# The first row tiles asked for by two queues, and the query weights in four transfers behind a hold

## The chip, the cores and the metric

The kernel runs on one core of one Trainium2 chip. The metric is the device time of one execution in microseconds. The kernel before took 1141.29 us, the median of three runs (1140.83 to 1142.23).

## The reference: what is computed

The input is x, 2 x 2048 rows of 512 float32 values. Two sublayers follow each other, each as x = x + layernorm(f(layernorm(x))).

The first, f, is an attention over 64 fixed latent keys with 16 heads of 32 values:

```
Q = h @ Wq.T + bq ;  V = h @ Wv.T + bv
logits = Q . latent / sqrt(32)              (64 for each head and row)
the best 4 of the 64, softmax over these 4, sum of their latent rows
out = (that sum + V) @ Wo.T + bo
```

The second is a gated expert layer of 2048 hidden values, silu(h @ Wu.T) * (h @ Wg.T), then @ Wd.T. Its three weight matrices are made ternary first: scale = mean(|W|) over the whole matrix, W = clip(round(W / scale), -1, 1) * scale. So every piece of such a matrix has to be read once for its scale before any piece of it can be used.

## The kernel before, in words

The 4096 rows are worked on in eight blocks of 512 rows, each of four tiles of 128 rows. All weights are loaded once and stay on the chip. While block b goes through the experts on TensorE, the attention of block b + 1 is worked in between by all engines. The start is different: nothing is there yet. Its order is written out by hand in FIRST_STEPS (line 36 on), a list of step names that is carried out from left to right. The table STEPS (line 856) says which function each name calls. The tile framework does not reorder anything; each engine takes its instructions in the order in which the steps issue them, and waits by semaphores.

What happens in the first 70 us, with the names that are used below:

- load_x(0) (line 129) asks for the four row tiles of block 0, 256 KB each, by SyncE's queue. Then one transfer for wq, the query weights (1024 KB, line 161), follows.
- Sixteen matmuls of ones (line 186) keep TensorE busy from the start. Their results go to at_psum, a PSUM pool of two buffers, and are not used.
- ast t takes the statistics of a row tile on VectorE (bn_stats and bn_aggr, lines 249 and 250). ars computes the reciprocal deviation on GpSimd (lines 256 and 257). aap t normalizes the tile on VectorE (line 276). atr t transposes it on TensorE in four pieces (line 286). acp t copies the transposed tile from PSUM to hT, by ScalarE for tiles 0 to 2 and by VectorE for tile 3 (lines 568 to 571).
- hold (line 852) stands behind ast0 in the list. It writes one column of lk by VectorE and then calls load_weights (line 163), which asks by SyncE's queue for lk, the biases, wv, lv, bo, the row tiles of block 1, and then the raw expert weights in pieces: eight of raw_u, four of raw_g, wo, four of raw_g, ten of raw_d. Because the first of these transfers writes lk, it waits for that VectorE write, and all the others stand behind it in the same queue.
- q c makes query tile c on TensorE (line 577, four matmuls over wq) into acc_psum, a pool of four buffers. qc copies it out on ScalarE (line 592) after bh, which copies bo (line 650). l makes the logits (line 602), lc copies them (line 610).
- su, sg, sd i sum the absolute values of one raw piece on ScalarE (line 206). tot adds the sums up on TensorE (line 214), sc makes the scale on VectorE, rd rounds a piece on GpSimd, and sgu, sgg and the like take its sign on ScalarE (line 237).
- m and r find the best four logits of a head on VectorE (lines 385 to 397), e and n make the weights of them.

There is one more order to know of. The transfers share eight queue semaphores in turn, so a transfer may have to wait until the one eight places before it has landed.

Of the kernel before, what the change touches and what calls it, by code (L numbers as in the profile page):

```python
# [17 lines left out]
P = 128  # L18
# [14 lines left out]


FIRST_STEPS = """
ast0 hold ast1 ars0_2 ast2 ars2_3 ast3 ars3_4 aap0 aap1 atr0 aap2 atr1 acp0 aap3 atr2 acp1 atr3 acp2 acp3 q0 bh
q1 qc0 bl nst0 l0 nst3 qc1 su0 nst1 v0 lc0 nst2 lc1 nrs su2 m1 su3 m0 l1 su1 r0 q2 lc2 su5 nap0
e0 r1 su6 ntr0 qc2 q3 ncp0 nap3 su7 nap1 nap2 sg1 n0 sg2 ob0 ob1 m2 ob2 e1 v1 qc3 n1 lc3 sg4 r2
t0 t1 tc0 ob3 tc1 sg5 m3 ntr2 e2 ntr1 ncp2 r3 y0 ncp1 l2 yc0 sg7 o3_0 n2 e3 o2_0 sd0 n3 v3 lc5
# [19 lines left out]
def latent_attention_ternary_glu(  # L59
# [15 lines left out]
    nc = tc.nc  # L75
    NT, D = x_in.shape
    E = wuT.shape[1]
    DC = D // P
# [18 lines left out]
    def at_psum(name):  # L97
        return ps_at.tile([P, 512], F32, tag="at", name=name)
# [11 lines left out]
    def transposed(which, b, name, dtype):  # L110
        return work.tile([P, DC, TB], dtype, tag=f"{which}{b % 2}", name=name, bufs=1)
# [17 lines left out]
    def load_x(b):  # L129
        x_tiles[b] = []  # L130
        for t in range(TT):
            xt = work.tile([P, D], F32, tag="x", name=f"x_{b}_{t}", bufs=2 * TT)
            r = b * TB + t * P
            nc.sync.dma_start(out=xt, in_=x_in[r : r + P, :])
            x_tiles[b].append(xt)


# [8 lines left out]
    def load_up(n, src, pieces):  # L146
        for i in pieces:
            k, h = halves[i]
            nc.sync.dma_start(
                out=raw[n, i], in_=src[k * P : (k + 1) * P, h * CH : (h + 1) * CH]  # L150
            )

    load_x(0)
    wq = wpool.tile([P, DC, D], F32, name="wq")
    wv = wpool.tile([P, DC, D], F32, name="wv")
# [2 lines left out]
    bo_sb = wpool.tile([P, D], F32, name="bo_sb")  # L158
    lk = wpool.tile([P, DC, 2 * L], F32, name="lk")
    lv = wpool.tile([P, H // 2, HP], F32, name="lv")  # L160
    nc.sync.dma_start(out=wq, in_=wqT.rearrange("(c p) n -> p c n", p=P))

    def load_weights():
        nc.sync.dma_start(out=lk, in_=latk)
        nc.sync.dma_start(out=bqv_sb, in_=bqv)
        nc.sync.dma_start(out=wv, in_=wvT.rearrange("(c p) n -> p c n", p=P))
        nc.sync.dma_start(out=lv, in_=latv)
        nc.sync.dma_start(out=bo_sb, in_=bo.to_broadcast([P, D]))
        load_x(1)
        load_up("u", wuT, (0, 2, 3, 1, 5, 6, 7, 4))  # L170
        load_up("g", wgT, (1, 2, 4, 5))
        nc.sync.dma_start(out=wo, in_=woT.rearrange("(c p) n -> p c n", p=P))
        load_up("g", wgT, (7, 6, 0, 3))
        for i in (0, 2, 3, 6, 7, 9, 8, 1, 5, 4):
            rows = 2 * P if i < 6 else P
            r = i * 2 * P if i < 6 else 12 * P + (i - 6) * P
            nc.sync.dma_start(
                out=raw["d", i].rearrange("p (c n) -> p c n", n=D),
                in_=wdT[r : r + rows, :].rearrange("(c p) n -> p c n", p=P),
            )  # L180
# [2 lines left out]
    both = work.tile([P, 2, P], F32, tag="hid", name="ones", bufs=2)  # L183
    ones = both[:, 0, :]
    nc.vector.memset(ones, 1.0)
    for i in range(16):
        nc.tensor.matmul(at_psum(f"ones_{i}")[:, :P], lhsT=ones, rhs=ones, start=True, stop=True)
    ident = wpool.tile([P, P], F32, name="ident")
    make_identity(nc, ident)
# [93 lines left out]
    def transpose_row(h, name, psum=at_psum):  # L283
        pt = psum(f"pt_{name}")
        for c in range(DC):
            nc.tensor.transpose(pt[:, c * P : (c + 1) * P], h[:, c * P : (c + 1) * P], ident)
        return pt.rearrange("p (c k) -> p c k", k=P)
# [252 lines left out]
    class FirstAttention(Attention):  # L540
# [19 lines left out]
        def a_trans_pe(self, t):  # L560
            if self.hT is None:
                self.hT = transposed("X", self.b, f"hT_{self.b}", F32)
            self.pt = getattr(self, "pt", {})
            self.pt[t] = transpose_row(self.rows.pop(("a", t)), f"a{self.b}_{t}")

        def a_copy(self, t):
            dst, src = self.hT[:, :, t * P : (t + 1) * P], self.pt.pop(t)
            if self.b == 0 and t == 3:
                nc.vector.tensor_copy(dst, src)
            else:  # L570
                nc.scalar.copy(dst, src)
# [277 lines left out]
        return work.tile([P, TB], F32, tag=tag, name=f"qT_0_{c}", bufs=2)  # L849


    def hold_weights():
        nc.vector.memset(lk[:, 0, 0:1], 0.0)
        load_weights()

    STEPS = {
        "ast": A.a_stats,
# [6 lines left out]
        "l": A.l_pe,  # L864
        "lc": A.l_copy,
        "hold": hold_weights,
        "m": A.m,
        "r": A.r,
# [151 lines left out]
    for b in range(NB):  # L1020
# [5 lines left out]
        for e in range(EC):  # L1026
            if e == 4 and 0 < b < NB - 1:
                load_x(b + 1)
# [136 lines left out]
```

## Time and profile before

| what | us |
|---|---|
| median of three runs | 1141.29 |
| the profiled execution, its whole time | 1141.65 |
| its span, first to last instruction | 1139.9 |
| TensorE busy | 1126.4 |
| first transpose of block 0 on TensorE (line 286) | 9.21 |
| first query matmul (line 577) | 12.48 |
| wq asked for, and us to landing | 2.57, 7.8 |
| the matmul that adds up raw_g's sums (line 214) | 69.15 |

Times in the views are microseconds from the start of the span. PE is TensorE's matmul, PEld its weight load, DVE is VectorE, ACT ScalarE, POOL GpSimd and SPq SyncE's queue. A row of the timeline gives start, length, engine, line, operation, what it writes and reads, its shape and how many such stood together; the bracket behind it is the idle time of the engine before it and what ended that. In the chain of waits each row is one link on the way back from the last instruction of the kernel: start, length, and the engine and line, or the transfer, in which the time passed. TensorE's granted clock is 0.999 of full in the whole span, in this profile.

### The profile page before, as it was taken

The numbers are of one execution on the slowest core, as the hardware profiler recorded it, in microseconds if no ns is written. First come the engines' busy times: TensorE is split into PE (matmuls) and PEld (weight loads), VectorE is DVE, ScalarE is ACT, GpSimd is POOL, SyncE is SP. The second block draws the span as 40 slices with busy tenths as digits, with TensorE's granted clock in tenths as the row PEclk, the third lists the DMA queues.
The fourth block names the chain that finished last, engine by engine and source line by source line (L and its number), as shares of the span: only waits on it lengthen the run. The fifth ranks groups of instructions, "written<-read, shape, count | busy, mean of one in ns | idle before, by whom it ended". The sixth has DMA issues, their size and how long they took to land.

```text
span 1139.9 us, 14491 instructions
## 1 busy us (share of the span) xinstructions
PE 1126.4 (99%) x4602; PEld 770.4 (68%) x4602; DVE 835.8 (73%) x2952; ACT 412.1 (36%) x715; POOL 164.8 (14%) x204
## 2 busy tenths in 40 slices
PE   8999999999999999999999999999999999999997
PEld 5547666767667665776657766586675766758885
DVE  5978968687866887678877778678786787846435
ACT  4985542332233332333214333153322433224223
POOL 1057003110032000320002200032001120020100
PEclk9999999999999999999999999999999999999999
DMA  9800221432213322222222222232321412102001
GB/s 350 305 0 21 73 94 41 108 120 84 83 52 97 102 86 81 73 76 93 93 74 75 83 95 96 60 103 65 117 68 56 111 65 93 63 3 74 37 1 37
DMA packets 98572, 97.16 MB, mean 85 GB/s; under 512 B 8384, under 2 KB 71104, under 8 KB 98496
## 3 DMA queue, kind: packets, MB, share of 16 engines
q1 hardware_dynamic: 98496, 96.24, 26.8%
q8 instruction: 36, 0.59, 0.2%
q14 instruction: 40, 0.33, 0.1%
HBM read 59.51 MB, written 36.70 MB: 84 GB/s over the span
## 4 chain that ended last, share of the span: by engine, by line
PE 94%; DVE 3%; ACT 1%; DMA 1%; issue 0%; SPq 0%; DVEq 0%; ACTq 0%
PE pg L716 20%; PE pu L716 19%; PE acc L759 19%; PE po L468 8%; PE pv L440 8%; PE pq L353 7%; PE pv L457 3%; PE pl L367 2%; PE pq L577 2%; PE po L668 1%; PE pv L622 1%; DMA hT<-far_a 1%; DMA x<-in_x 0%; PE pl L602 0%; DVE left L393 0%; ACT tern_g L237 0%
## 5 line engine op out<-in xcount | busy, mean ns | idle before, releaser
L716 PE MATMUL pg<-hT_f,tern_g 128*128 128x512 f32 x512 | 207.6, 405 | 0.0
L716 PE MATMUL pu<-hT_f,tern_u 128*128 128x512 f32 x512 | 204.7, 401 | 0.0
L759 PE MATMUL acc<-tern_d,hi 128*128 128x512 f32 x512 | 203.4, 397 | 0.0
L759 PE MATMUL acc<-tern_d,lo 128*128 128x512 f32 x512 | 199.8, 390 | 0.9 <-DVE lo L749 0.8
L716 PE MATMUL pg<-lT_f,tern_g 128*128 128x512 f32 x512 | 199.6, 390 | 0.0
L716 PE MATMUL pu<-lT_f,tern_u 128*128 128x512 f32 x512 | 198.9, 389 | 0.0
L725 ACT ACTIVATE h<-pu,columns 128x512 f32<-128x512 f32 x128 | 87.0, 680 | 203.5 <-PE pu L716 203.5
L728 DVE SCALAR_TENSOR_TENSOR h<-h,pu 128x512 f32<-128x512 f32 x128 | 85.9, 671 | 93.7 <-ACT h L725 93.7
L744 ACT CAST hi<-h 128x512 fp32r<-128x512 f32 x128 | 79.1, 618 | 199.2 <-DVE h L733 199.1
L733 DVE TENSOR_TENSOR h<-h,pg 128x512 f32<-128x512 f32 x128 | 86.4, 675 | 63.5 <-PE pg L716 62.3
L759 PEld LDWEIGHTS acc<-tern_d,hi 128*128 128x128 f32 x512 | 96.1, 188 | 32.9 <-issue 13.6
L716 PEld LDWEIGHTS pg<-hT_f,tern_g 128*128 128x128 f32 x512 | 96.1, 188 | 25.3 <-issue 1.4
L716 PEld LDWEIGHTS pu<-hT_f,tern_u 128*128 128x128 f32 x512 | 96.1, 188 | 25.1 <-issue 3.1
L759 PEld LDWEIGHTS acc<-tern_d,lo 128*128 128x128 f32 x512 | 96.1, 188 | 22.9 <-DVE lo L749 2.2
L716 PEld LDWEIGHTS pu<-lT_f,tern_u 128*128 128x128 f32 x512 | 96.2, 188 | 22.6 <-issue 3.1
L716 PEld LDWEIGHTS pg<-lT_f,tern_g 128*128 128x128 f32 x512 | 96.2, 188 | 21.7 <-issue 2.9
L749 DVE TENSOR_TENSOR lo<-h,hi 128x512 fp32r<-128x512 f32 x128 | 89.9, 702 | 23.1 <-ACT hi L744 23.1
L440 PE MATMUL pv<-hT,wv 128*128 128x512 f32 x224 | 100.7, 592 | 0.3 <-ACT w L375 0.3
L393 DVE MATCH_REPLACE8 left<-m,w 128x64 f32<-128x64 f32 x512 | 100.3, 210 | 0.0
L468 PE MATMUL po<-wo,attnT 128*128 128x512 f32 x224 | 97.3, 592 | 0.0
L353 PE MATMUL pq<-hT,wq 128*128 128x512 f32 x192 | 86.7, 594 | 0.5 <-DMA hT<-far_a 0.2
L468 PEld LDWEIGHTS po<-wo,attnT 128*128 128x128 f32 x224 | 42.5, 190 | 50.8 <-issue 48.6
(141 smaller groups left out, 1310.7 us busy)
## 6 DMA issues: line engine op xcount, KB each, us to landing
dz<-z SPq DMA_DIRECT2D x56, 256.0 KB, 2.0
wT<-dz SPq DMA_DIRECT2D x224, 64.0 KB, 1.9
x<-in_x SPq DMA_DIRECT2D x32, 256.0 KB, 3.7
out_x<-x SPq DMA_DIRECT2D x31, 256.0 KB, 2.0
far_f<-zf SPq DMA_DIRECT2D x28, 256.0 KB, 2.8
hw<-far_f SPq DMA_DIRECT2D x56, 128.0 KB, 3.4
xa<-in_x SPq DMA_DIRECT2D x6, 1024.0 KB, 5.3
far_a<-za SPq DMA_DIRECT2D x24, 256.0 KB, 2.9
```

The source lines that it names most:

```text
L353: nc.tensor.matmul(pq, lhsT=wq[:, k, c * P : (c + 1) * P], rhs=self.taken(k), start=(k == 0), stop=(k == DC - 1),)
L393: nc.vector.match_replace(left[:, g, :], m8[:, g, :], w[:, g, :], TAKEN)
L440: nc.tensor.matmul(self.pv[c], lhsT=wv[:, k, c * P : (c + 1) * P], rhs=self.ordered(k), start=(k == 0), stop=False,)
L457: nc.tensor.matmul(self.pv[c][pr * HP : (pr + 1) * HP, :], lhsT=lv[:, 2 * c + pr, :], rhs=self.wT.pop(2 * c + pr), start=False, stop=True, ...
L468: nc.tensor.matmul(self.po[t], lhsT=self.attnT[:, c, t * P : (t + 1) * P], rhs=wo[:, c, :], start=(c == 0), stop=(c == DC - 1),)
L716: nc.tensor.matmul(p, lhsT=tern[n, 2 * k + e // 8][:, (e % 8) * P : (e % 8 + 1) * P], rhs=self.parts[i][:, k], start=(k, i) == pairs[0], s ...
L725: nc.scalar.activation(self.h[e], self.pu[e], AF.Tanh, scale=half_u[0])
L728: nc.vector.scalar_tensor_tensor(self.h[e], self.h[e], 1.0, self.pu.pop(e), ALU.add, ALU.mult)
L733: nc.vector.tensor_tensor(self.h[e], self.h[e], self.pg.pop(e), ALU.mult)
L744: nc.scalar.copy(hi, self.h[e])
L749: nc.vector.tensor_tensor(lo, self.h.pop(e), self.hid[e][0].bitcast(F32), ALU.subtract)
L759: nc.tensor.matmul(self.acc[t], lhsT=part[:, t * P : (t + 1) * P], rhs=wd, start=(e == 0 and i == 0), stop=(e == EC - 1 and i == 1),)
```

## The change

Five edits, all in the first microseconds:

```
-ast0 hold ast1 ars0_2 ast2 ars2_3 ast3 ...
+ast0 hold0 ast1 ars0_2 ast2 hold1 ars2_3 ast3 ...
...
-            nc.sync.dma_start(out=xt, in_=x_in[r : r + P, :])
+
+            queue = nc.scalar if b == 0 and t % 2 else nc.sync
+            queue.dma_start(out=xt, in_=x_in[r : r + P, :])
...
-    nc.sync.dma_start(out=wq, in_=wqT.rearrange("(c p) n -> p c n", p=P))
-
-    def load_weights():
+    def load_weights(group):
+        if group == 0:
+            for k in range(DC):
+                nc.sync.dma_start(out=wq[:, k, :], in_=wqT[k * P : (k + 1) * P, :])
+            return
...
-    for i in range(16):
+    for i in range(20):
         nc.tensor.matmul(at_psum(f"ones_{i}")[:, :P], lhsT=ones, rhs=ones, start=True, stop=True)
...
-            self.pt[t] = transpose_row(self.rows.pop(("a", t)), f"a{self.b}_{t}")
+            psum = acc_psum if self.b == 0 and t >= 2 else at_psum
+            self.pt[t] = transpose_row(self.rows.pop(("a", t)), f"a{self.b}_{t}", psum)
...
-            if self.b == 0 and t == 3:
+            if self.b == 0 and t == 2:
                 nc.vector.tensor_copy(dst, src)
...
-    def hold_weights():
-        nc.vector.memset(lk[:, 0, 0:1], 0.0)
-        load_weights()
+    def hold_weights(group):
+        nc.vector.memset((lk if group else wq)[:, 0, 0:1], 0.0)
+        load_weights(group)
```

Row tiles 1 and 3 of block 0 are asked for by ScalarE's queue, where they stand ahead of its first activation table load; tiles 0 and 2 stay on SyncE's. The query weights come in four transfers of 256 KB, one for each 128 rows of the matrix, and the first of them waits for a VectorE write to wq that stands behind tile 0's statistics (hold0). The other weights wait for the write to lk, which now stands behind tile 2's statistics (hold1). There are 20 matmuls of ones, not 16. The transposes of tiles 2 and 3 go to acc_psum, and of the copies to hT it is tile 2's that VectorE makes, so that ScalarE makes tile 3's. Nothing else differs on any engine but the numbers of the queue semaphores.

More of the change, by code (lines that the diff above doesn't have):

```diff
@@ L35 @@
 FIRST_STEPS = """
-ast0 hold ast1 ars0_2 ast2 ars2_3 ast3 ars3_4 aap0 aap1 atr0 aap2 atr1 acp0 aap3 atr2 acp1 atr3 acp2 acp3 q0 bh
+ast0 hold0 ast1 ars0_2 ast2 hold1 ars2_3 ast3 ars3_4 aap0 aap1 atr0 aap2 atr1 acp0 aap3 atr2 acp1 atr3 acp2 acp3 q0 bh
 q1 qc0 bl nst0 l0 nst3 qc1 su0 nst1 v0 lc0 nst2 lc1 nrs su2 m1 su3 m0 l1 su1 r0 q2 lc2 su5 nap0
```

## The prediction

> **What bounds the kernel now.** I read the page first, then the chain of waits over the first 60 us, the timeline of the first 13 us, the DMA view, and last the places where an engine starts exactly when something lands.
>
> ```profile
> PE 1126.4 (99%) x4602; PEld 770.4 (68%) x4602; DVE 835.8 (73%) x2952; ACT 412.1 (36%) x715; POOL 164.8 (14%) x204
> ```
>
> TensorE is busy 1126.4 of 1139.9 us, so all its idle time is 13.5 us, and nothing in this diff shortens its useful work. The chain of waits, first 60 us (start, length, what):
>
> ```profile
> 1.63 5.27 DMA x<-in_x
> ...
> 6.92 0.71 DVE st_a L249
> ...
> 9.21 0.64 PE pt_a L286 x4
> ...
> 12.48 7.10 PE pq L577 x16
> ```
>
> The start waits for the third row tile: asked for at 1.63, landed at 6.90. From 12.48 on the chain is TensorE. The timeline of VectorE:
>
> ```profile
> 3.43 0.69 DVE L249 BATCH_NORM_STATS2 st_a<-x 128x6 f32<-128x512 f32 x1 [2.45 <-DMA x<-in_x]
> ...
> 4.29 0.06 DVE L853 MEMSET lk<- 128x1 f32 x1
> ...
> 6.92 0.69 DVE L249 BATCH_NORM_STATS2 st_a<-x 128x6 f32<-128x512 f32 x1 [1.75 <-DMA x<-in_x]
> ```
>
> Tile 0 is there at 3.4 and tile 1 by 4.26, then VectorE waits 1.75 us for tile 2. The wait is in transfers, not in their issue: the DMA view gives 2.7 us to landing for the first tile, 5.4 for those asked for last, and wq, asked for at 2.57, takes 7.8, so lands at 10.4. In the stages table the 16 DMA engines are busy 1.03 and 0.92 of the time from 4 to 6 us yet move only 281 and 219 GB/s, against 405 later (us, PE, PEld, DVE, ACT, POOL, clock, DMA share, GB/s):
>
> ```profile
> 5.00:6.00 1.00, 1.00 (x10) 0.99 (x9) 0.17 (x1) 0.00 (x0) 0.65 (x2) 1.00 0.92 219
> ...
> 20.00:40.00 20.00, 20.00 (x90) 10.46 (x86) 18.72 (x113) 18.66 (x38) 1.21 (x2) 1.00 1.03 405
> ```
>
> So packets of the last tiles and the first of wq are slow together, and the weight stream then runs full until 49 us. That stream matters more than the start:
>
> ```profile
> 20.21 1.05 ACT L206 ACTIVATE junk<-raw_u 128x1024 bf16<-128x1024 f32 x1
> ...
> 22.36 1.11 DVE L385 MAX8 m<-w 128x8 f32<-128x64 f32 x8 [0.60 <-ACT w L610]
> ...
> 43.37 1.07 ACT L206 ACTIVATE junk<-raw_d 128x1024 bf16<-128x1024 f32 x1
> ...
> 69.15 0.30 PEld L214 LDWEIGHTS tot_g<-sums_g,ones 128*128 128x128 f32 x2 [0.85 <-ACT junk L206]
> ```
>
> The first raw_u is asked for at 11.51 and takes 8.4, so lands at 19.9: ScalarE's sum over it starts 0.3 later. The first raw_d (31.52 + 11.7) lands at 43.2: its sum starts 0.15 later. VectorE waits at 22.36 for the ScalarE copies behind that first sum and then never again until 69.58, where it waits for tot_g; ScalarE at 64.18 waits for VectorE, and at 69.15 TensorE, which has done its earlier work at 69.12, takes tot_g just as ScalarE delivers (69.10). Three engines are level at 69 us. TensorE can be early there only if ScalarE and VectorE are, and these only if raw_u and raw_d land earlier.
>
> **The change, part by part.** I write G for how much sooner the first query matmul starts, and s for how much sooner the weight stream lands.
>
> Row tiles on two queues. SyncE issues four tiles at about 0.45 us each (1.81 in all); now two each, so the last is issued at 1.2 instead of 2.1. The issuing moves ahead of ScalarE's table load (1.28 us at 0.71), which ends some 0.9 later, at 2.9; its first copy is at 9.87, so that costs nothing. The Trainium skill ("DMA: Bandwidth & Descriptors", Issuing engines are not separate DMA queues) says that all queues end in the same 16 DMA engines and that several issuers save the sequencer's time only. The row agrees in part: a 256 KB tile deep in the stream lands 0.7 after the one before (1024 KB of next rows: 17.9, then 18.6), longer than the 0.45 of an issue. By the rule this part earns 0; by the issue times at most 0.9. I take 0 for the first tiles and count on it only to have all four in flight by 1.6. It can cost: tile 0 shares with tile 1, up to 0.4 (half a tile) on the first landing, and the hold follows from it.
>
> wq held. It is now released by a memset that follows tile 0's statistics, where lk's memset stands now (4.29; SyncE issues at 4.37). Then no wq packet is in flight while the four tiles land. Four tiles at 0.7 from the first bytes (the table by 0.5 us has 57 GB/s in 1.5:2.0, so about 1.7) give 4.5 to 5.0 for the last, in place of 7.6. VectorE then goes through its four statistics without a pause: 0.83 each (3.43 to 4.26), 3.43 + 3.3 = 6.75 instead of 8.5. GpSimd's small operations (0.2 to 0.8) run beside. First normalized tile: 7.2, the fourth at 6.75 + 2.04 = 8.8.
>
> Four more ones matmuls. 17 passes took 2.61 us, so 8 more cost 8 x 0.154 = 1.2, and they end at 8.2 instead of 7.0. Before, TensorE then idled 2.21 us, so they were covered; now the first normalized tile is there at 7.2 and the transposes wait for 8.2. This eats 1 us of the 1.9.
>
> Transposes in four PSUM tiles. Third and fourth no longer wait for ScalarE's copies (0.22 us). Four tiles at 1.08 per two: 8.2 + 2.2 = 10.4; then ScalarE's copy of the last (0.58, where VectorE took 0.69) 11.0, and the first query matmul at 11.1. G = 12.48 - 11.1 = 1.4; 1.8 if the passes overlap as those of the transposes do, 0.3 if the tiles are not sooner and only the copies are. The pool of four is used again by the third query tile, long after.
>
> wq in four. Four issues of 0.4 hold SyncE 1.3 us longer than one. A rule speaks against it: the same page (Rules for kernel authors) wants 1 MiB or more per DMA, and its fit (2.0 us plus bytes, for GpSimd's transfers) would make four in a row an estimated 8 us of fixed cost. The row: queued 256 KB tiles land 0.7 apart, four 2.8, and one 1 MB transfer takes about as long; so in a full queue splitting costs 0. I take the row.
>
> The stream behind. The new wait stands on SyncE, and behind it there stand, in order, the other wq quarters, lk (held until tile 2's statistics, about 5.9, and free to go at 6.1 when SyncE is through with wq), the biases, wv, the next rows, raw_u, raw_g and raw_d. All of them move with it. A queue semaphore is used again after eight transfers, so bo and three next rows now wait for a quarter of wq each, where one row waited for the whole (issued at 10.43 as wq landed); quarters land before that, so this costs nothing. Lower end for s: the DMA engines stand empty from 4.7 or 5.0 to the first wq bytes; issue to first bytes took 1.0 (0.72 to 1.7), so these come at 5.4 to 5.7 and the hole is 0.4 to 1.0 us; if the slow packets come again, s = -0.3 to -1.0. Upper end: without them wq takes 1 MB at 370 GB/s, 2.8 us, from 5.5: 8.3, with a spread of the engines about 9, in place of 10.4: s = +1.4. I take s = +0.6, nearer the middle: fewer transfers in flight should mean fewer slow packets, but a cold queue has slow ones too.
>
> Sum: the shift at 69 us is the smaller of G and (slack + s), slack being 0.15 from the raw_d row (0.3 from raw_u). min(1.4, 0.15 + 0.6) = 0.75. After 69.15 TensorE runs to 94 us without a gap and VectorE and ScalarE follow it, so it lasts to the end. The profiled execution took 1141.65 (span 1139.9 plus 1.75 around it), 0.36 above the median of the runs, 1141.29; from it 1140.9, from the median 1140.5.
>
> **Rivals.**
> - The hole decides (slower). Mechanism: the hold empties the DMA engines at about 5 us and the slow packets return once wq starts. For it: the stream has no slack afterwards (405 GB/s, share 1.03), so a hole is never made good, and G does not help, since ScalarE waits at raw_u and raw_d. Against: in 4 to 6 us about 0.3 MB less than at full rate moved, which is as much as the hole. Price: s = -0.65, so 0.65 - 0.15 = +0.5: 1141.8, to 1142.4 for s = -1.3. It decides once the last of wq lands later than 10.4 + 0.15, about 10.6.
> - The stream comes clean (faster). s = 1.4 or more, G is the limit: -1.4, 1139.9; with G = 1.8, 1139.5. For it: the slow packets fall in just the two microseconds in which tiles and wq overlap, and later transfers of wq's shape (wv, wo) move at full rate. Against: one profile cannot tell what made them slow; the first microseconds of the queue would look the same.
> - The change doesn't do what it says. The tiles land no sooner because two queues share the engines, or lk's hold slips; s and G near 0: 1141.2.
>
> **How the numbers follow.** The likeliest case (s 0.2 to 1.0, 1140.1 to 1140.9): 0.43. Clean stream, 1139.9: 0.22. Hole, 1141.8: 0.25. Nothing, 1141.2: 0.10. A measurement of this kernel can tell about 0.2%, 2.3 us, from no change, and every case's centre lies inside. Beyond it: faster takes a clean stream with an earlier first tile and a cost of slow packets that was larger in the timed runs than in the profile, half of that case: 0.11. Slower takes a hole with late tiles on the second queue, so that lk and all behind it slip by 2.5 us: 0.10. Rest 0.79. The range 1139.4 to 1142.4 takes in the three centres and the ends of G and s.
>
> **What would show it.** Right: tile 2's statistics start by 5.2 without a wait for DMA; the ones end at 8.2 and the transposes follow without a gap; the first query matmul starts at 10.7 to 11.1; wq lands before 10.4 and the first raw_d before 43.2, and tot_g is reached earlier than 69.15 by the same amount. Wrong: ScalarE idle before raw_u or raw_d sums longer than before; the first query matmul waiting for wq instead of for the copies; tot_g later although the query matmul is sooner. The prediction fails on its size if landings and end do not move together.

## The result, and the profile after

The changed kernel takes 1143.59 us (median of 22 runs, 1142.65 to 1144.78); the kernel before took 1142.14 beside it (22 runs, 1140.83 to 1143.50). The ratio is 1.0014, with a 95% interval of 1.0008 to 1.0019: slower by about 1.5 us. That is small, but the interval does not reach 1. The time lies outside the predicted range (1139.4 to 1142.4), on the slow side; 1140.5 was predicted. Of the distance to it 0.85 us is the base: the prediction reckoned from 1141.29, and the kernel before took 1142.14 here. Reckoned from 1141.29 the ratio gives 1142.9, which is outside too. The profiled execution took 1143.16 us, its span 1141.2 (before 1139.9).

TensorE's busy time on the page is 1128.3 us, 1.9 more, of which the ones are 1.8 (40 passes in 7.76 us, where 32 took 5.97).

The timeline of VectorE shows the front working as it was meant to. The four statistics run without a wait between them, but they begin at 4.20 instead of 3.43, because tile 0 lands later:

```profile
4.20 0.69 DVE L253 BATCH_NORM_STATS2 st_a<-x 128x6 f32<-128x512 f32 x1 [3.22 <-DMA x<-in_x]
...
5.06 0.06 DVE L858 MEMSET wq<- 128x1 f32 x1
...
6.66 0.69 DVE L253 BATCH_NORM_STATS2 st_a<-x 128x6 f32<-128x512 f32 x1
6.68 0.06 DVE L858 MEMSET lk<- 128x1 f32 x1
```

TensorE's timeline: ones to 8.79, transposes from 8.63, first query matmul at 11.29, 1.19 us sooner than before (12.48):

```profile
1.03 7.76 PE L191 MATMUL ones<-ones 128*128 128x128 f32 x40 [1.03 <-DVE ones L189]
8.63 1.98 PE L290 MATMUL pt_a<-ident,h_a 128*128 128x128 f32 x16
11.29 1.99 PE L582 MATMUL pq<-hT,wq 128*128 128x512 f32 x4 [0.67 <-ACT hT L576]
```

The start is won, and yet the kernel is slower. The stages table says why (the last two columns are the busy share of the DMA engines and GB/s). The memset releases wq at 5.06, when the tiles have all but landed, and in the microsecond after that the DMA engines move 4 GB/s:

```profile
5.00:6.00 1.00, 1.00 (x7) 1.00 (x6) 0.97 (x5) 0.00 (x0) 0.00 (x0) 1.00 0.01 4
6.00:7.00 1.00, 1.00 (x8) 0.97 (x7) 0.96 (x4) 0.00 (x0) 0.88 (x2) 1.00 0.78 195
...
9.00:10.00 1.00, 1.00 (x12) 0.96 (x10) 0.55 (x1) 0.68 (x2) 0.32 (x1) 1.00 0.92 300
10.00:11.00 1.00, 0.61 (x6) 0.37 (x4) 0.69 (x1) 0.74 (x2) 0.00 (x0) 1.00 1.02 212
11.00:12.00 1.00, 0.71 (x2) 0.47 (x3) 0.00 (x0) 0.43 (x2) 0.00 (x0) 1.00 0.82 244
...
20.00:40.00 20.00, 19.28 (x76) 9.58 (x74) 19.09 (x109) 18.61 (x38) 1.21 (x2) 1.00 1.03 407
```

The same stretches before (5 to 6 us stands in the prediction):

```profile
6.00:7.00 1.00, 1.00 (x8) 0.80 (x6) 0.08 (x1) 0.00 (x0) 0.26 (x1) 1.00 0.96 352
...
9.00:10.00 1.00, 0.80 (x7) 0.79 (x8) 0.97 (x3) 0.13 (x1) 0.92 (x2) 1.00 1.05 375
10.00:11.00 1.00, 0.78 (x7) 0.47 (x6) 0.55 (x1) 0.94 (x2) 0.01 (x1) 1.00 1.06 408
11.00:12.00 1.00, 0.65 (x6) 0.41 (x4) 0.31 (x1) 0.78 (x2) 0.00 (x0) 1.00 1.04 403
```

There are two weak stretches, not one: 5 to 7 us, and 9 to 12 us, where the share is 0.82 to 1.02 and the rate only 212 to 300 GB/s. From 0 to 16 us the mean is 253 GB/s where it was 303, so (303 - 253) x 16 = 0.8 MB less; at 407 GB/s that is 2.0 us of loading. After 16 us both kernels load at 406 to 407, so nothing makes it good: the first raw_u lands at 20.87 (before 19.86), the first raw_d at 45.10 (43.25).

A landing is the last of the sixteen arrivals that the trace notes for a transfer, as many as there are DMA engines. On the mean of the sixteen the first raw_u is 2.05 later than before and the first raw_d 2.08, as the bytes say. The last of the sixteen is 1.01 later at raw_u and 1.85 at raw_d. In between, at the eighth piece of raw_u (landings at 28.55 and 30.75, elsewhere 1.3 apart), one of the sixteen fell 1.0 us behind the others, while the loading ran at full rate, and it stayed behind: raw_d's fifteenth arrival is at 44.04, against 43.08 before. So about half of the 1.85 is one late engine's in this execution. It alone is not what makes the kernel slow: in the profiles of f4 and g1 below, which hold wq too, the last arrival is only 0.1 and 0.3 behind the fifteenth, and the first raw_d still lands 1.66 and 1.45 later than before.

ScalarE's timeline then has waits for two sums, where before had none, and a longer one for bo:

```profile
16.91 0.62 ACT L655 CAST bias<-bo_sb 128x512 fp32r<-128x512 f32 x1 [5.48 <-DMA bo_sb<-in_bo]
20.89 1.06 ACT L210 ACTIVATE junk<-raw_u 128x1024 bf16<-128x1024 f32 x1 [1.75 <-DMA raw_u<-in_wuT]
...
45.18 1.06 ACT L210 ACTIVATE junk<-raw_d 128x1024 bf16<-128x1024 f32 x1 [1.70 <-DMA raw_d<-in_wdT]
```

Before, ScalarE waited for bo alone:

```profile
15.89 0.62 ACT L650 CAST bias<-bo_sb 128x512 fp32r<-128x512 f32 x1 [3.91 <-DMA bo_sb<-in_bo]
```

The chain of waits, which before was TensorE's from 12.48 on but for 3.2 us of ScalarE at 37.5, is now one of DMAs up to 45 us, and from there to 70.7 one of ScalarE and VectorE (start, length, what):

```profile
7.89 6.99 DMA wv<-in_wvT
14.90 7.24 DMA raw_u<-in_wuT
22.16 11.16 DMA raw_g<-in_wgT
33.33 11.77 DMA raw_d<-in_wdT
45.14 0.04 issue
45.18 1.15 ACT junk L210 x2
```

It ends at the same place as before, with TensorE waiting for ScalarE (tot_g at 69.15 before):

```profile
70.76 0.30 PEld L218 LDWEIGHTS tot_g<-sums_g,ones 128*128 128x128 f32 x2 [0.97 <-ACT junk L210]
```

tot_g is 1.61 us later, and the end of the last matmul of the program 1.60 later (1134.59 after 1132.99). That the two agree is partly chance: from tot_g to that end it is 1063.84 and 1063.83 us in these two profiles, but 1064.22 to 1065.33 in the twelve below (the last section says where it goes).

### The profile page after: what moved, and what is told of

It is laid out like the page before. It is cut to its first block, busy times and chain, and to the rows that moved or that the text cites. A ratio compares the mean times of both kernels' runs of the same rounds, so it can differ in the third digit from the quotient of the medians.

```text
span 1141.2 us, 14510 instructions
## 1 busy us (share of the span) xinstructions
PE 1128.3 (99%) x4610; PEld 772.8 (68%) x4610; DVE 835.3 (73%) x2953; ACT 412.0 (36%) x715; POOL 164.9 (14%) x204
## 4 chain that ended last, share of the span: by engine, by line
PE 89%; DVE 5%; DMA 4%; ACT 1%; issue 0%; SPq 0%; DVEq 0%; ACTq 0%
PE pg L721 20%; PE pu L721 19%; PE acc L764 19%; PE po L472 8%; PE pv L444 8%; PE pq L357 7%; PE pv L461 2%; PE pl L371 2%; DMA raw_d<-in_wdT 1%; DVE left L397 1%; DMA raw_g<-in_wgT 1%; DVE m L389 1%; DMA raw_u<-in_wuT 1%; DMA wv<-in_wvT 1%; PE pq L582 1%; DMA hT<-far_a 1%
```

## The experiments

My first theory after the result: the hold leaves the DMA engines dry, everything behind is late, and ScalarE's sums, which run in their written order, pass it on. The rivals: the second queue costs (tile 0, and with it the hold, is late); the split of wq costs; the new front of TensorE costs by itself; the landings differ by chance between programs. All numbers of one row below are from that kernel's own profile, the ratio is against the kernel before on the same chip (the e, f and g runs were on three chips). "GB/s" is the mean of the first 16 us.

| kernel | wq held | others released behind | GB/s | first raw_d | tot_g | ratio, 95% interval |
|---|---|---|---|---|---|---|
| before | no | tile 0 | 303 | 43.25 | 69.15 | 1 |
| after | yes | tile 2 | 253 | 45.10 | 70.76 | 1.0014 (1.0008 to 1.0019) |
| e1 | yes | tile 2 | 270 | 44.46 | 70.12 | 1.0006 (0.9998 to 1.0014) |
| e2 | no | tile 2 | 268 | 45.37 | 71.04 | 1.0007 (0.9999 to 1.0015) |
| e3 | yes | tile 2 | 262 | 44.69 | 70.37 | 1.0008 (1.0000 to 1.0016) |
| e4 | yes | tile 2 | 246 | 45.93 | 70.97 | 1.0007 (1.0001 to 1.0014) |
| f1 | no | not held | 314 | 42.39 | 68.06 | 0.9992 (0.9986 to 0.9998) |
| f2 | no | tile 0 | 318 | 42.25 | 67.96 | 0.9989 (0.9983 to 0.9996) |
| f3 | no | tile 0 | 308 | 42.46 | 68.13 | 1.0000 (0.9993 to 1.0008) |
| f4 | yes | tile 2 | 250 | 44.91 | 70.58 | 1.0009 (1.0002 to 1.0017) |
| g1 | yes | tile 0 | 251 | 44.70 | 70.37 | 1.0011 (1.0002 to 1.0019) |
| g2 | no | tile 0 | 312 | 42.83 | 68.49 | 0.9994 (0.9985 to 1.0003) |
| g3 | no | tile 0 | 311 | 42.80 | 68.49 | 0.9996 (0.9987 to 1.0005) |
| g4 | no | tile 1 | 291 | 43.45 | 69.12 | 1.0003 (0.9994 to 1.0012) |

The intervals of e1, e2 and e3 reach 1, so for these three the profile says more than the time. In it the rate is a safer sign than the first raw_d and tot_g, which hang on the slowest engine: the last arrival of raw_d is 1.79 us behind the fifteenth in e2, 1.48 in e4, 1.05 in the changed kernel, 0.88 in g4, and 0.1 to 0.7 in the other ten.

**e1, all four tiles on SyncE's queue.**

```
-            queue = nc.scalar if b == 0 and t % 2 else nc.sync
+            queue = nc.sync
```

> The changed kernel with all four row tiles of block 0 back on SyncE's queue; all else as changed. Theory A (the hold empties the DMA engines and everything behind lands later): the hold stays, so the loss stays for the most part; tile 0 lands at 3.4 instead of 4.2, the hold is released 0.8 sooner, first raw_d lands 0.5 to 0.8 sooner than in the changed kernel (45.1 to 44.4), time 0.5 to 0.8 below it, still 0.6 to 1.0 above the kernel before. Theory B (the loss is the second queue's, which made the first tile late): the whole loss goes, time within 0.3 us of the kernel before.

1143.28 us against 1142.38. Tile 0 lands at 3.49 again, wq is asked for at 4.46, and the dry stretch shrinks (139 GB/s in 5 to 6 us), but the first raw_d is still 1.2 later than before. The second queue makes the hold start later; without it about two thirds of the delay stays (1.21 of 1.85). By the times e1 can be told neither from the changed kernel nor from the one before.

**e2, wq not held** (the other weights still behind tile 2).

```
-        nc.vector.memset((lk if group else wq)[:, 0, 0:1], 0.0)
+        if group:
+            nc.vector.memset(lk[:, 0, 0:1], 0.0)
```

> The changed kernel without the VectorE write that holds wq: the four quarters are asked for right behind the tiles; lk's hold, two queues, 20 ones and PSUM places as changed. Theory A: wq's first bytes follow the tiles without a hole, wq lands at about 10.4 or sooner instead of 10.6 and, above all, the next transfers without a cold start: first raw_d at 43.2 to 43.7, time 0 to 0.5 above the kernel before, or below it if the sooner query matmul counts. Theory B: tile 0 is as late as in the changed kernel, nothing is won by more than 0.3 us.

1143.28 against 1142.38, although wq is complete at 8.60, two microseconds sooner than in the changed kernel. The first theory, that wq's hold is the cause, missed here. The stages table of e2 shows what took its place: the loading is full until 7 us and falls behind wq, because lk is now asked for at 7.11 and wv at 7.95.

```profile
5.00:6.00 1.00, 1.00 (x8) 0.97 (x7) 0.97 (x3) 0.00 (x0) 0.00 (x0) 1.00 1.03 397
6.00:7.00 1.00, 1.00 (x10) 0.95 (x9) 0.93 (x5) 0.00 (x0) 0.56 (x2) 1.00 1.07 414
7.00:8.00 1.00, 1.00 (x9) 0.95 (x9) 0.97 (x5) 0.00 (x0) 0.83 (x3) 1.00 0.76 283
8.00:9.00 1.00, 0.90 (x8) 0.69 (x8) 1.00 (x3) 0.00 (x0) 0.83 (x3) 1.00 0.79 237
9.00:10.00 1.00, 0.98 (x9) 0.75 (x8) 0.55 (x2) 0.87 (x2) 0.64 (x1) 1.00 0.76 107
```

The hole has moved from 5 to 7 us to 7 to 10 us, and is as large: against 407 GB/s it lacks 0.6 MB in either place. So either hold alone makes one. Much of the late raw_d in this profile is one engine's, as said; that the second hold costs rests on the rate and on the times of f2, below.

**e3, wq in one held transfer of 1024 KB.**

```
-            for k in range(DC):
-                nc.sync.dma_start(out=wq[:, k, :], in_=wqT[k * P : (k + 1) * P, :])
+            nc.sync.dma_start(out=wq, in_=wqT.rearrange("(c p) n -> p c n", p=P))
```

> The changed kernel with wq as one held transfer of 1024 KB instead of four of 256 KB. Theories A and B: within 0.4 us of the changed kernel. Theory C (the splitting costs): 1 us or more sooner, back to the kernel before.

1143.58 against 1142.38. wq lands at 11.26 and the hole lasts from 5 to 7.5 us, so the split is not what costs.

**e4, the first sums of raw_u and raw_d later in the written order.** The sum su0 goes from ahead of nst1 to behind nrs, and sd0 from behind o2_0 to behind m5.

```
-q1 qc0 bl nst0 l0 nst3 qc1 su0 nst1 v0 lc0 nst2 lc1 nrs su2 ...
+q1 qc0 bl nst0 l0 nst3 qc1 nst1 v0 lc0 nst2 lc1 nrs su0 su2 ...
-... e3 o2_0 sd0 n3 v3 lc5
-lc4 m5 sd2 ...
+... e3 o2_0 n3 v3 lc5
+lc4 m5 sd0 sd2 ...
```

> The changed kernel with two sums moved in the order of steps: the sum over the first raw_u behind the two copies of the logits that VectorE waits for, and the sum over the first raw_d behind the next two. If the loss reaches the end through ScalarE, which stands at those two sums while the copies behind them are ready (the changed profile has 1.75 and 1.70 us of such waits), VectorE starts 0.3 sooner at 23.0 and does not wait 0.9 at 46.8: time 0.8 to 1.3 below the changed kernel. If the late landings act by another way (sums needed at 70 and 82, TensorE's own wait at the start): no change beyond 0.3 us.

1143.57 against 1142.38. The ratio, 1.0007 with an interval that overlaps the changed kernel's, leaves open whether the order won anything. ScalarE's timeline of e4 shows that a later place only hands the wait to the sums behind:

```profile
46.02 1.06 ACT L210 ACTIVATE junk<-raw_d 128x1024 bf16<-128x1024 f32 x1 [0.71 <-DMA raw_d<-in_wdT]
...
47.37 1.06 ACT L210 ACTIVATE junk<-raw_d 128x1024 bf16<-128x1024 f32 x1 [0.21 <-DMA raw_d<-in_wdT]
```

Its first raw_d landed 0.83 later than in the changed kernel and tot_g came 0.21 later, so the place is worth some 0.6 us of slack; the whole stream is late, not two transfers.

After these four the theory became: any stretch in which the queue runs dry or nearly so comes back at the first raw_d, whichever hold makes it. The next four tell that from the front and from chance.

**f1, neither hold.** The memset line is left out.

> The changed kernel with neither memset: the four transfers of wq and all later weights are asked for as fast as SyncE's queue takes them, behind the tiles. Dry-queue theory (each stretch before 15 us in which little is in flight comes back whole at the first raw_d, and ScalarE's in-order sums wait for it): e2 only moved the hole from wq (5 to 6.5 us) to lk (7 to 10.5 us), so without both the loading runs at about 400 GB/s from 3 us on; the first raw_u lands about 18.5, the first raw_d about 42 to 42.5 (before 43.25, after 45.10), tot_g's matmuls start at 68.5 to 69.2, and the kernel takes 0.3 us less to 0.1 us more than the one before. Front theory (the twenty ones, the other accumulators and copies cost by themselves, the loading is a bystander): tot_g stays at 70.5 or later and the kernel stays 1.0 to 1.5 us slower than the one before whatever the loading does. Chance theory (single DMA engines stall late in the stream, unrelated to the start): the first raw_d lands past 44.5 here too.

1141.02 against 1141.74: faster than the kernel before. tot_g came sooner than the interval expected.

**f2, wq not held, and the others released behind tile 0,** as before had it; the two queues, the four transfers and the new front stay.

```
-ast0 hold0 ast1 ars0_2 ast2 hold1 ars2_3 ast3 ...
+ast0 hold0 hold1 ast1 ars0_2 ast2 ars2_3 ast3 ...
...
-        nc.vector.memset((lk if group else wq)[:, 0, 0:1], 0.0)
+        if group:
+            nc.vector.memset(lk[:, 0, 0:1], 0.0)
```

> The changed kernel with wq not held and the other weights released behind the statistics of tile 0, the places that the kernel before has, so that the four-way split, the two queues and the new front are all that is left of the change. Dry-queue theory: wq lands by 8.6 as in e2, a short gap may stay ahead of lk because tile 0's statistics now end at 5.2 where lk is asked for, which is before wq has drained (8.6), so no hole; first raw_d at 42.5 to 43.3, the kernel between 0.4 us under and 0.2 us over the one before. Front theory: 1.0 to 1.5 us slower. Chance theory: raw_d past 44.5.

1140.82 against 1141.74: the lowest ratio of all (f1's interval overlaps it), faster than the kernel before by more than the expected 0.4, with the first raw_d sooner than the expected 42.5. Its stages table has no hole where e2 had one; the only edit between the two is the place of lk's memset, 5.1 instead of 7.1 us:

```profile
7.00:8.00 1.00, 1.00 (x9) 0.94 (x8) 0.96 (x4) 0.00 (x0) 0.83 (x3) 1.00 1.05 404
8.00:9.00 1.00, 1.00 (x10) 0.84 (x9) 0.92 (x3) 0.19 (x1) 0.83 (x3) 1.00 1.10 391
9.00:10.00 1.00, 0.71 (x8) 0.47 (x5) 0.64 (x2) 0.89 (x2) 0.33 (x1) 1.00 1.00 373
```

All that ScalarE waits for between 15 and 71 us in f2 is other engines, no DMA (line waited for, us, times, longest):

```profile
ACT qT L597 <- PE pq L582: 3.3, 2, 2.7
ACT wT L643 <- PE pw L637: 1.1, 1, 1.1
ACT top L406 <- DVE top L401: 0.3, 1, 0.3
```

and its chain of waits is TensorE's again as before, beginning 1.2 us sooner:

```profile
11.29 7.13 PE pq L582 x16
```

From there to tot_g it is 56.67 us, as in the kernel before, so in f2 tot_g is sooner by just what the first query matmul is (1.19). By that sum f2's gain needs the new front beside the early loading, but f2 with the old front was not run.

**f3, the kernel before with TensorE's new front alone** (twenty ones, acc_psum for tiles 2 and 3, VectorE copying tile 2).

> The kernel before with the front of TensorE's work alone taken from the change: twenty ones, the transposes of tiles 2 and 3 in the other accumulators, VectorE copying tile 2 and ScalarE tile 3; every transfer asked for as before. Dry-queue theory: the loading is that of before (first raw_d 43.0 to 43.6), the first query matmul starts at 11.6 to 12.5, and the kernel is within 0.4 us of the one before. Front theory: 1.0 to 1.5 us slower than the one before, tot_g at 70 or later.

1141.97 against 1141.74, no difference. The front does no harm. In its profiled execution the loading happened to run better than in before's (308 GB/s, first raw_d at 42.46) although it asks for the same transfers, and tot_g came at 68.13; the timed runs do not show that gain, and of its 1.02 us only 0.09 are left at the last matmul of the same profile.

**f4, the changed kernel with the old front:** those three edits undone.

> The changed kernel with the front of the kernel before (sixteen ones, one accumulator set for the transposes, VectorE copying tile 3): what is left is the two queues, the four transfers of wq and the two holds. Dry-queue theory: hole from 5 to 6.5 us again, first raw_d at 44.5 to 45.5, tot_g at 70.2 to 71, 1.0 to 1.6 us slower than the one before. Front theory: within 0.4 us of the one before.

1143.24 against 1141.74: with the old front the loss is still there, so it lies in the loading.

**g1, wq held as in the changed kernel, the others released behind tile 0.**

```
-ast0 hold0 ast1 ars0_2 ast2 hold1 ars2_3 ast3 ...
+ast0 hold0 hold1 ast1 ars0_2 ast2 ars2_3 ast3 ...
```

> The changed kernel with both memsets behind the statistics of tile 0, so that wq is still held but lk and the rest no longer wait for tile 2's statistics. Dry-queue theory: wq's requests alone take SyncE from 5.1 to 6.9 us, so lk is asked for as late as in the changed kernel and the dry stretch from 5 to 6.5 us stays; first raw_d 44.3 to 45.3, tot_g at 70 to 71, 0.9 to 1.6 us slower than the one before. The rival reading, that it is the second release (lk behind tile 2) that costs and wq's hold is harmless: like f2, 0.5 to 1.2 us faster than the one before.

1143.58 against 1142.20. lk is asked for at 7.08 (7.01 in the changed kernel): wq's four requests stand ahead of it on SyncE and are themselves released at 5.1, so one hold makes all of it late.

**g4, wq not held, the others released behind tile 1.**

```
-ast0 hold0 hold1 ast1 ars0_2 ast2 ars2_3 ...
+ast0 hold0 ast1 hold1 ars0_2 ast2 ars2_3 ...
```

> The step between f2 and e2: wq not held, the other weights released behind tile 1's statistics, about 6.1 us (f2: 5.1, e2: 7.1). Dry-queue theory as a threshold: wq drains at 8.4 to 8.6, and lk's first packets follow its request by 1.0 to 1.6 us, so a request at 6.2 to 6.4 still reaches the engines before they run dry; no hole, first raw_d at 42.2 to 43, tot_g at 68 to 68.8, 0.4 to 1.0 us faster than the one before. If the cost grew evenly with the delay instead, it would lie half way between f2 and e2: tot_g about 69.5, within 0.3 us of the one before.

1142.19 against 1142.20; tot_g at 69.12. The threshold missed: a part of the cost is there already, although lk was asked for (6.02) and wv too (6.87) before wq had drained (8.30). The stages table of g4 shows the weak stretch:

```profile
7.00:8.00 1.00, 1.00 (x10) 1.00 (x8) 0.96 (x4) 0.00 (x0) 0.83 (x3) 1.00 1.04 389
8.00:9.00 1.00, 1.00 (x10) 0.88 (x10) 0.94 (x3) 0.16 (x1) 0.83 (x3) 1.00 0.85 197
9.00:10.00 1.00, 0.71 (x8) 0.47 (x6) 0.61 (x2) 0.91 (x2) 0.35 (x1) 1.00 0.96 264
```

So an empty queue is not needed; a short one is enough here. By its rate, half way between f2 and e2 (291, between 318 and 268), and by its time g4 agrees with the other reading, a cost that grows evenly with the delay. See the last section.

**g2, f2 with one queue; g3, f2 with wq in one transfer.**

> f2 with all four tiles on SyncE's queue: what the second queue is worth once no queue runs dry. Tile 0 lands at 3.4 to 3.6 instead of 4.2, but wq is asked for some 0.9 us later behind two more requests of SyncE; tot_g at 67.9 to 68.7, within 0.4 us of f2, that is 0.4 to 1.0 us faster than the one before. If the second queue is what made f2 fast: back at the time of the one before.

> f2 with wq in one transfer of 1024 KB: what the four transfers are worth once no queue runs dry. One request instead of four frees SyncE 1.3 us sooner, lk is asked for at its release, and the bytes are the same: tot_g at 67.8 to 68.6, within 0.3 us of f2, 0.5 to 1.2 us faster than the one before. If the split is what made f2 fast: within 0.3 us of the one before.

1141.45 and 1141.34 against 1142.20. Both expectations held for tot_g (68.49), and both intervals include no change, so what the second queue and the split are worth beside f2 can't be told from these runs.

## Why the prediction was wrong, point by point

**The path to tot_g: right. From there to the end: in part luck.** I took the shift at 69 us as the smaller of G and (slack + s), with a slack of 0.15 at the first raw_d, and said that it lasts to the end. The landing was 1.85 later, and -1.85 + 0.15 = -1.70; tot_g came 1.61 later. In the twelve kernels other than before and e4, tot_g starts 25.66 to 25.71 us after the first raw_d lands; in before it is 25.90, so the slack was 0.23 (-1.85 + 0.23 = -1.62), and in e4, where the sum was moved, it is 25.04. I had also read the chain of before as TensorE's from 12.48 on; 3.2 us of it, from 37.5, are ScalarE's, which changes nothing in the sum. f2 shows the other side of the smaller-of rule: there s allows, and tot_g moves by G. That the shift lasts to the end came out as 1.60, but by luck of these two profiles; in the others 0.4 to 1.5 us more went by between tot_g and the end.

**The front: nearly right, and without effect in this kernel.** The first query matmul came at 11.29 (11.1 said), so G was 1.19, not 1.4. The ones ended at 8.79 (8.2 said). That is not the price of the added passes: in both profiles the passes begin at about 0.21 us each and go on at about 0.14, and the step came after 16 passes before and after 26 in the changed kernel. In the other kernels 40 passes ended anywhere from 7.78 to 8.81. The granted clock reads 1.00 in the rows, so why the step moves stays open. f3 shows that the front by itself moves nothing measurable, and f4 that the loss is there without it, as the formula has it: G counts only when s allows.

**Tile 0: bound too small.** I allowed 0.4 for sharing with tile 1. It landed at 4.18, 0.78 later, and at 3.49 in e1 with one queue. The memset for wq therefore came at 5.06, not 4.3, and SyncE's request at 5.15, not 4.4. The last tile landed at 5.55, where I had 4.5 to 5.0.

**The step that failed: "I take s = +0.6".** I weighed a hole of 0.4 to 1.0 us against the slow packets that should go, and took the side of the gain because fewer transfers in flight should mean fewer slow packets. The runs showed s = -1.0 at raw_u and -1.85 at raw_d, the second beyond the -1.3 of my worst hole (0.9 of it is the one late engine). Against before, from 5 to 7 us 372 KB less were moved, 0.9 us at 407 GB/s: that is the hole, at the upper end of its bound. From 9 to 12 us another 430 KB less, 1.06 us: this second stretch I had not counted. 131 KB were won from 3 to 5 us and 112 lost from 12 to 16. So the reason for the gain failed: the slow packets of before, at 4 to 6 us, did not go but stand at 9 to 12 us now, where engines busy 0.82 to 1.02 of the time moved 212 to 300 GB/s.

**Which edit.** I put the cost on wq's hold alone and let lk's second hold go free, because lk would wait for SyncE anyway. With wq held that is so (g1 against the changed kernel: 1.0011 and 1.0014). But e2 against f2 shows that the second hold by itself costs too (1.0007 and 0.9989, whose intervals do not overlap, and 268 and 318 GB/s). The four corners:

| | others behind tile 0 | others behind tile 2 |
|---|---|---|
| wq not held | f2, 0.9989 | e2, 1.0007 |
| wq held | g1, 1.0011 | after, 1.0014 |

One corner is fast; the other three cannot be told apart by their intervals. The two costs do not add, since with wq held lk is late already (g1).

**Rivals.** "The hole decides" had the mechanism and the sign, with a price of 0.5 to 1.2 where the runs gave 1.5; the second stretch, which it did not count, can make the difference. Its deciding point (last of wq later than 10.6) was met, at 10.63, but by luck: in e2 wq is complete at 8.60 and the stream is late all the same. What decides is the stream behind wq. "The stream comes clean" is what f2 does, with the hold taken out. The split costing nothing was right: with one transfer wq lands no sooner (11.26 in e3 for 10.63, 10.05 in g3 for 8.43), and the times show no gain. The Trainium skill's rule that several issuers share the same DMA engines ("DMA: Bandwidth & Descriptors", Issuing engines are not separate DMA queues) also stood up: by it the second queue should earn nothing beyond issue time, and g2 against f2 shows no gain that can be told from noise.

## What to carry to other kernels

Where the loading is what the kernel later waits for, ask first what will be in flight in each microsecond while a hold lasts; here a hold that was to free the early tiles was paid for with every byte behind. Holding transfers back to make an early one land sooner needs enough queued to carry the DMA engines over release, request and first packets. In g4 and f2, which differ in the place of one hold alone, wv was asked for 2.25 us ahead of its turn and the rate fell, and 3.3 us ahead and it did not. When two waits can each empty the same queue, take both away before judging either: one edit at a time would have acquitted both.

## What the runs showed of the hardware that was not expected

After a dry stretch the loading does not come back at once. In e3 wq is asked for at 5.47, the first packets come at 6.5, and until 8.0 the stages table has 168, 115 and 254 GB/s per half microsecond, then 389: 1.0 us to the first packet, then 1.5 us at 179 GB/s on the mean, less than half of 407.

A transfer seems to need a lead. Counting as lead the time from the request for wv (1024 KB) to the landing of what stands before it, wv came at 383 to 415 GB/s with a lead of 4.1 to 5.7 us (f1, g2, f4, g1, f3, before), at 400 with 3.3 (f2), but at 253 and 251 with 2.25 and 1.91 (g4, e2). The changed kernel (306 with 3.6), e1 (362 with 3.9), g3 (365 with 4.8), e3 (308 with 4.2) and e4 (316 with 4.0) do not fit a sharp bound, so this is a correlation, and what makes the packets slow stays open; so does the second weak stretch of the changed kernel as far as its cause goes.

Programs that ask for the same transfers land them up to 1.0 us apart: the first raw_d at 44.91, 45.10 and 45.93 in f4, the changed kernel and e4, and at 43.25 and 42.46 in before and f3. One engine that falls behind is a large part of it: raw_d's fifteenth arrival is at 44.81, 44.04 and 44.46 in the first three. Such an engine lost 0.5 to 1.6 us within one transfer at full rate in e1, e2, e4, f1, f2, g4 and the changed kernel, fast and slow ones alike; why stays open. A single profile can't settle a step of half a microsecond here.

Part of a gain can also be lost far from the change. In every later block the first query matmul starts within 0.04 to 0.26 us of the landing of hT, which comes back through DRAM. TensorE idled 0.8 us before it at 494.7 in f2, where the profile names hT, and 0.85 us at 772.0 in f3. At these two blocks the idle times add up to 0.03 us in the profile of before, 0.6 in the changed kernel's and 0.9 to 1.4 in the other twelve. So of f2's 1.19 us at tot_g, 0.81 were left at the last matmul (1132.18 against 1132.99) in the profiled executions.
